# A segment-maximum product on the full array in place of two column halves

## The chip, the cores and the metric

One core of one Trainium2 chip runs the whole kernel. The time is the device time of one execution, in microseconds (us). Each matmul engine instruction is seen in the profile as a weight load (PEld) and a matmul (PE); an f32 product is two such pairs.

## The reference

A graph layer over 12,500 nodes and 400,000 edges, the edges sorted by their target node. `h` is the layer norm of `x` clipped at zero; every edge passes source features, target features and its own features through a two-layer perceptron, and each node takes the maximum over its incoming edges.

```python
h = jnp.maximum(_layernorm(x, axis=-1), 0.0)
e_feat = jnp.concatenate([h[src], h[dst], edge_attr], axis=-1)   # 400000 x 96
v = jax.nn.relu(e_feat @ W1 + b1) @ W2 + b2                      # 96 -> 64 -> 32
x_cand = jax.ops.segment_max(v, dst, num_segments=12500)
out = x + jnp.maximum(x_cand, h)
```

## The kernel before

The edges are cut into four stripes (NS = 4) and each stripe into 196 chunks of C = 512 edges. A chunk is worked on for all four stripes at once; since the target nodes are sorted, the edges of one stripe in one chunk fall into a window of W = 32 consecutive nodes, whose first node is known beforehand.

The main loop takes two chunks a pass (c and c + 1), 98 passes. While it finishes chunks c and c + 1, it gathers the source rows of chunks a = c + 2 and b = c + 3. In a chunk, 12 groups of 128 source rows come by indirect DMAs issued by POOL (line 156, 24 a pass), and four groups come by `tile`: 14 matmuls of a one-hot matrix against the node table `hs` (line 240), a masked product and a maximum on DVE (lines 244 and 245). `to_features` transposes both kinds into `ht` on DVE (lines 258 and 261). A gathered row group lies in one of 24 buffers, three groups each, and a buffer comes free with the transpose.

The first layer sums three products into the four PSUM tiles `ph` (line 502: edge features, target windows, source rows, each a 64-row half of the array); ACT applies the relu (line 557); the second layer is line 573, written into two column halves of a PSUM tile `pv`. DVE scans along the edges of each stripe with add and max (line 580), so that at the last edge of every node stands that node's maximum.

`leave_1` and `leave_2` take these maxima out. `lasts` (line 470) makes, for every block of 128 edges (J = 4 of them), a 0/1 matrix `last` of 128 edges by 4 stripes by 32 window places: one where the edge is the last of its node. `leave_1` transposes the scan result to edges by (4 stripes x 32 features) (line 478) and adds the bias (line 480), giving `so`. `leave_2` multiplies `last` with `so` (line 488), so that each window place gets its node's maximum, copies the result to `wo` on ACT (line 492) and writes four pieces of 32 nodes by 32 features to `top_d` (line 496). Stripes 0 and 2 go to one table, 1 and 3 to the other, and the end of the kernel takes the larger.

Every engine but POOL works in the order written out by hand. On PE a pass reads: tile(a, 0), source-row products, tile(a, 1), tile(a, 2), edge products, second layer, window products, the deferred `leave_2` of the odd chunk of the pass before, tile(a, 3), transposes, tile(b, 0), `leave_2` of chunk c, tile(b, 1), transposes, tile(b, 2), tile(b, 3). The PSUM tiles `pv` come from one pool of three buffers that `tile`, the second layer, `leave_1` and `leave_2` use in turn. SP's queue carries the window loads `qw` (line 457), the edge features and the write-outs of `wo`, in the order of the program.

Of the kernel before, what the change touches and what calls it, by code (L numbers as in the profile page):

```python
# [8 lines left out]
F32 = mybir.dt.float32  # L9
# [14 lines left out]
P = 128  # L24
N = 12500
E = 400000
D = 32
# [3 lines left out]
NS = 4  # L31
W = 32
C = 512
J = C // P
# [33 lines left out]
def gnn_kernel(ctx, tc, x, src, src_mm, src_t, dst, dst_ext, lo, lo_c, ends_b, edge_attr, weights, w1, w2, b2, out):  # L68
# [19 lines left out]
    nc = tc.nc  # L88
# [7 lines left out]
    top_d = [dram.tile([NP, D], F32, name=f"top_d{k}") for k in range(2)]  # L96
# [66 lines left out]
    early_ps = ctx.enter_context(tc.tile_pool(name="early_ps", bufs=1, space=PSUM))  # L163
# [265 lines left out]
    with tc.tile_pool(name="edges", bufs=3) as pool, tc.tile_pool(name="edges_ps", bufs=1, space=PSUM) as ps:  # L429
# [37 lines left out]
        def lasts(c):  # L467
            last = pool.tile([P, J, NS, W], F32, name="last", bufs=2)
            at = ats[c // BLOCK].rearrange("p (s c) j -> p s c j", s=NS)[:, :, c % BLOCK].rearrange("p s j -> p j s")
            nc.vector.tensor_tensor(last, count_ps[:, None, None, :].to_broadcast([P, J, NS, W]),  # L470
                                    at[:, :, :, None].to_broadcast([P, J, NS, W]), op=ALU.is_equal)
            return last

        def leave_1(c, sm):

            px = early_ps.tile([P, C], F32, name="pv", bufs=3).rearrange("p (j q) -> p j q", j=J)
            for j in range(J):
                nc.tensor.transpose(px[:, j, :], sm[:, j * P:(j + 1) * P], ident)
            so = pool.tile([P, J, P], F32, name="so", bufs=2)
            nc.vector.tensor_tensor(so, px, b2r[:, None, :].to_broadcast([P, J, P]), op=ALU.add)  # L480
            return so

        def leave_2(c, so, last):

            pw = early_ps.tile([P, C], F32, name="pv", bufs=3)[:, :2 * D]
            for j in range(J):
                for g in range(2):
                    nc.tensor.matmul(pw[g * 2 * W:(g + 1) * 2 * W],  # L488
                                     last[:, j, 2 * g:2 * g + 2].rearrange("p s w -> p (s w)"),
                                     so[:, j, g * 2 * D:(g + 1) * 2 * D], start=(j == 0), stop=(j == J - 1))  # L490
            wo = pool.tile([P, 2 * D], F32, name="wo")
            nc.scalar.activation(wo, pw, AF.Copy)  # L492
            _, base = windows.pop(c)
            for s in range(NS):
                g = slice(s * W, (s + 1) * W)
                nc.sync.dma_start(top_d[s % 2][bass.ds(base[s], W), :], wo[g, s % 2 * D:(s % 2 + 1) * D])

        def into_ph(ph, pairs, start, stop):
            for x, (w, e) in enumerate(pairs):
# [35 lines left out]
        for c in range(0, NCH, 2):  # L535
# [32 lines left out]
            last = [lasts(c)]  # L568
            ph = edges_into(a)
            pv = [early_ps.tile([P, C], F32, name="pv", bufs=3) for x in range(2)]  # L570
# [15 lines left out]
            so = leave_1(c, sms[0])  # L586
            last.append(lasts(c + 1))
            tile(b, 0)
            to_features(b, 0)
            one_hots(a + 2, 0, 2)  # L590
            leave_2(c, so, last[0])
            tile(b, 1)
            to_features(b, 1)
            so = leave_1(c + 1, sms[1])
# [11 lines left out]
            if c == (NB - 1) * BLOCK:  # L606
# [7 lines left out]
                nc.tensor.matmul(bp, worst, ones, start=True, stop=True)  # L614
                nc.vector.tensor_copy(general_i, bp)
            leave = lambda c=c + 1, so=so, last=last[1]: leave_2(c, so, last)
        leave()

# [154 lines left out]
```

## Time and profile before

| what | value |
|---|---|
| median of 3 runs | 4055.93 us (4045.58 to 4070.74) |
| the profiled execution, its time | 4066.76 us |
| its span, first to last instruction | 4065.0 us |
| mean granted PE clock | 0.939 |
| busy PE, PEld, DVE, ACT, POOL | 3500.2, 2584.2, 2232.7, 1106.1, 2257.0 us |
| line 488 on PE: 3136 matmuls | 166.1 us busy, 232 ns each |
| line 492 on ACT: 196 copies | 43.8 us busy, 223 ns each |

Busy time counts an engine as busy while an instruction of it is in flight. Matmuls overlap, so the mean time of one is longer than the distance from one to the next; where that distance matters, it is read from the starts in the timeline. An idle time is put down to the event that ended it; "issue" means that the profile shows no such event.

### The profile page before, as it was taken

Reading aid. Unit: us, or ns where it says so; the run is one execution under the profiler, and the core shown is the slowest. Engines: PE = TensorE matmul, PEld = TensorE weight load, DVE = VectorE, ACT = ScalarE, POOL = GpSimd, SP = SyncE. Lnnn points to the kernel's source line nnn. Section 1 sums busy time; section 2 is a strip of 40 time slices with the busy share of each in tenths; the row PEclk is TensorE's granted clock in tenths of the full one; section 3 lists DMA queues with packets and bytes.
Section 4 is the critical chain, followed back from the end, with each engine's and each line's share of the span. In section 5 each row is a group of like instructions: output and inputs, shape, how many; then the busy total and the mean of one; then the engine's idle time right before and its main releaser. Section 6 shows DMA issues by size and latency. Waiting matters only on the chain. (4 is left out here: it accounts for less than half of the span.)

```text
span 4065.0 us, 52812 instructions
## 1 busy us (share of the span) xinstructions
PE 3500.2 (86%) x18053; PEld 2584.2 (64%) x18053; DVE 2232.7 (55%) x3876; ACT 1106.1 (27%) x1795; POOL 2257.0 (56%) x2376
## 2 busy tenths in 40 slices
PE   4688889888888898888988888998888889998896
PEld 3466666666666666666666666666666666666665
DVE  4355556555555555555555555555555555655555
ACT  3122222222222222222222232322222223222231
POOL 6555555555555556555555555555555555555550
PEclk7799999999999999999999999999999999999998
DMA  5122212211222122111322222222122222211221
GB/s 189 46 48 65 52 44 55 68 43 44 54 65 49 44 51 69 46 44 46 71 49 47 62 58 47 44 70 52 44 46 66 53 47 49 70 48 44 57 59 50
DMA packets 188622, 229.27 MB, mean 56 GB/s; under 512 B 117549, under 2 KB 159933, under 8 KB 175550
## 3 DMA queue, kind: packets, MB, share of 16 engines
q10 hardware_dynamic: 26692, 110.63, 8.7%
q1 hardware_dynamic: 86618, 76.67, 7.7%
q0 software_dynamic: 75040, 38.57, 6.3%
q8 instruction: 143, 2.34, 0.2%
q14 instruction: 129, 1.06, 0.1%
HBM read 211.76 MB, written 13.85 MB: 56 GB/s over the span
## 5 line engine op out<-in xcount | busy, mean ns | idle before, releaser
L156 POOL DMA_INDIRECT gh<-h_d,src_i x2345 | 2236.5, 954 | 1685.9 <-issue 619.2
L240 PE MATMUL pv<-hs,hot 128*128 128x448 f32 x10920 | 2434.7, 378 | 231.8 <-issue 166.7
L240 PEld LDWEIGHTS pv<-hs,hot 128*128 128x128 f32 x10920 | 2077.6, 194 | 509.9 <-issue 258.1
L244 DVE TENSOR_TENSOR one<-pv,mask 128x448 f32<-128x448 f32 x780 | 478.3, 613 | 1590.8 <-remote 653.4
L557 ACT ACTIVATE hid<-ph,wt 128x512 f32<-128x512 f32 x392 | 254.6, 686 | 1498.2 <-PE ph L502 920.7
L209 DVE TENSOR_TENSOR hot<-kb,consts 128x1536 fp32r<-128x1536 f16 (+2 forms) x388 | 566.1, 1459 | 0.0
L245 DVE TENSOR_REDUCE gm<-one 128x32 f32<-128x448 f32 x780 | 483.6, 620 | 26.9
L219 ACT ACTIVATE hot<-away,ones 128x512 fp32r<-128x512 f32 x392 | 283.6, 724 | 337.3 <-issue 326.3
L580 DVE TENSOR_TENSOR_SCAN sm<-pb,sm,pv 128x512 f32<-128x512 bf16 x195 | 248.2, 1273 | 150.5 <-remote 114.7
L492 ACT ACTIVATE wo<-pv 128x64 f32<-128x64 f32 x196 | 43.8, 223 | 1052.8 <-PE pv L488 765.0
L573 PE MATMUL pv<-hid,wt 128*64 128x512 f32 x784 | 242.1, 667 | 62.2 <-issue 36.3
L488 PEld LDWEIGHTS pv<-so,last 128*64 128x64 f32 x3136 | 126.0, 140 | 250.7 <-issue 162.0
L488 PE MATMUL pv<-so,last 128*64 128x64 f32 x3136 | 166.1, 232 | 131.9 <-issue 121.7
L218 ACT ACTIVATE away<-kb,key_n 128x512 f32<-128x512 f16 x392 | 277.7, 708 | 0.0
L502 PE MATMUL ph<-ea,wt 64*128 64x512 f32 x784 | 233.8, 632 | 35.2 <-issue 29.8
L502 PE MATMUL ph<-ht,wt 64*128 64x512 f32 x784 | 209.7, 637 | 48.3 <-DVE ht L261 42.7
L258 DVE STREAM_TRANSPOSE ht<-gh 128x96 f32<-128x96 f32 x782 | 209.7, 268 | 0.0
L502 PE MATMUL ph<-of,qw 64*128 64x512 f32 x784 | 206.0, 635 | 2.8 <-issue 2.7
L573 PEld LDWEIGHTS pv<-hid,wt 128*64 128x64 f32 x784 | 57.1, 143 | 235.2 <-issue 161.4
L502 PEld LDWEIGHTS ph<-of,qw 64*128 64x128 f32 x784 | 71.9, 195 | 145.4 <-issue 139.3
L502 PEld LDWEIGHTS ph<-ea,wt 64*128 64x128 f32 x784 | 78.3, 188 | 129.5 <-issue 116.2
L502 PEld LDWEIGHTS ph<-ht,wt 64*128 64x128 f32 x784 | 65.2, 188 | 138.2 <-DVE ht L261 77.8
(78 smaller groups left out, 1014.1 us busy)
## 6 DMA issues: line engine op xcount, KB each, us to landing
ea<-in_edge_attr SPq DMA_DIRECT2D x49, 1024.0 KB
db<-in_dst_ext ACTq DMA_DIRECT2D x48, 1024.0 KB
gh<-h_d,src_i POOLq DMA_INDIRECT x2345
pb<-pen_d ACTq DMA_DIRECT2D x48, 512.0 KB
kb<-key_d ACTq DMA_DIRECT2D x47, 512.0 KB
qw<-q_d SPq DMA_DIRECT2D x784, 8.0 KB
top_d<-wo SPq DMA_DIRECT2D x784, 4.0 KB
top_d<-zero ACTq DMA_DIRECT2D x2, 1568.0 KB
```

Of the source, the lines that this page charges most:

```text
L156: nc.gpsimd.indirect_dma_start(out=parts[-1][:, i, :], out_offset=None, in_=h_d[:, :], in_offset=bass.IndirectOffsetOnAxis(ap=src_i[:, c, ...
L209: nc.vector.tensor_tensor(hot_of(c)[:, start:stop], keys[c][:, None, :].to_broadcast([P, n, MM * P]), key_ps[:, start:stop, None].to_broad ...
L218: nc.scalar.activation(away, keys[c], AF.Square, bias=key_n[:, k:k + 1])
L219: nc.scalar.activation(hot_of(c)[:, k], away, AF.Relu, bias=ones, scale=-1.0)
L240: nc.tensor.matmul(po, hot[:, k, e], hs[:, part, k].rearrange("p f a -> p (f a)"), start=(k == 0 and part == 0), stop=(k == A1 - 1 and par ...
L244: nc.vector.tensor_tensor(one, of_group, masks[c][:, m, None, :].to_broadcast([P, D, A0]), op=ALU.mult)
L245: nc.vector.tensor_reduce(mm_rows[c][:, m, :], one, axis=AX.X, op=ALU.max)
L488: nc.tensor.matmul(pw[g * 2 * W:(g + 1) * 2 * W], last[:, j, 2 * g:2 * g + 2].rearrange("p s w -> p (s w)"), so[:, j, g * 2 * D:(g + 1) * ...
L502: nc.tensor.matmul(ph[2 * x + k], w[g], e[g], start=start, stop=stop)
L557: nc.scalar.activation(hid[s], ph[s], AF.Relu, bias=b1c)
L573: nc.tensor.matmul(pv[x][k * 2 * D:(k + 1) * 2 * D], w2x, hid[2 * x + k], start=True, stop=True)
L580: nc.vector.tensor_tensor_scan(sm, loaded.pop(c + x)[2], pv[x], before, op0=ALU.add, op1=ALU.max)
```

## The change

`leave_2` is rewritten. Before, two products per block of 128 edges, each for a pair of stripes, with 64 stationary columns and 64 moving columns, write the lower and the upper half of a 128 x 64 result. After, one product per block takes all four stripes: 128 stationary columns (4 stripes x 32 places) and 128 moving columns (4 stripes x 32 features). Of the 128 x 128 result only the four 32 x 32 blocks on the diagonal, a stripe's places with the same stripe's features, are wanted; the others are copied along and not written out. `wo` becomes 128 x 128 and has two buffers in place of the pool's three. The products of the first and second layer, with their block-diagonal weights, are as before.

```diff
         def leave_2(c, so, last):
-            pw = early_ps.tile([P, C], F32, name="pv", bufs=3)[:, :2 * D]
+            pw = early_ps.tile([P, C], F32, name="pv", bufs=3)[:, :NS * D]
             for j in range(J):
-                for g in range(2):
-                    nc.tensor.matmul(pw[g * 2 * W:(g + 1) * 2 * W],
-                                     last[:, j, 2 * g:2 * g + 2].rearrange("p s w -> p (s w)"),
-                                     so[:, j, g * 2 * D:(g + 1) * 2 * D], start=(j == 0), stop=(j == J - 1))
-            wo = pool.tile([P, 2 * D], F32, name="wo")
+                nc.tensor.matmul(pw, last[:, j].rearrange("p s w -> p (s w)"), so[:, j],
+                                 start=(j == 0), stop=(j == J - 1))
+            wo = pool.tile([P, NS * D], F32, name="wo", bufs=2)
             nc.scalar.activation(wo, pw, AF.Copy)
             _, base = windows.pop(c)
             for s in range(NS):
                 g = slice(s * W, (s + 1) * W)
-                nc.sync.dma_start(top_d[s % 2][bass.ds(base[s], W), :], wo[g, s % 2 * D:(s % 2 + 1) * D])
+                nc.sync.dma_start(top_d[s % 2][bass.ds(base[s], W), :], wo[g, s * D:(s + 1) * D])
```

## The prediction

> **What bounds the kernel now.** I read the busy table first, then the groups of instructions, then the timeline of single passes, engine by engine, then a table by stage.
>
> ```profile
> PE 3500.2 (86%) x18053; PEld 2584.2 (64%) x18053; DVE 2232.7 (55%) x3876; ACT 1106.1 (27%) x1795; POOL 2257.0 (56%) x2376
> L488 PEld LDWEIGHTS pv<-so,last 128*64 128x64 f32 x3136 | 126.0, 140 | 250.7 <-issue 162.0
> L488 PE MATMUL pv<-so,last 128*64 128x64 f32 x3136 | 166.1, 232 | 131.9 <-issue 121.7
> ...
> L492 ACT ACTIVATE wo<-pv 128x64 f32<-128x64 f32 x196 | 43.8, 223 | 1052.8 <-PE pv L488 765.0
> ```
>
> By its share PE looks like the bound, and the edited product is 166 us of it, 4% of the span. The next table sets four passes of the main loop (two chunks each, from one tile(a, 0) to the next) side by side; columns are the stretch, its length, busy time (instructions) of PE, PEld, DVE, ACT and POOL, then PE clock, DMA share, GB/s.
>
> ```profile
> 1605.50:1650.30 44.80, 37.92 (x186) 28.26 (x186) 22.20 (x40) 10.90 (x18) 22.86 (x25) 0.89 0.28 68
> 1650.30:1687.70 37.40, 33.87 (x185) 25.34 (x184) 22.16 (x40) 11.21 (x18) 23.24 (x26) 1.00 0.17 34
> 2017.30:2056.80 39.50, 36.54 (x185) 25.96 (x185) 21.99 (x39) 11.20 (x18) 22.84 (x25) 0.96 0.31 74
> ...
> 3956.00:3988.60 32.60, 32.60 (x185) 25.04 (x184) 22.29 (x38) 10.88 (x18) 0.00 (x0) 1.00 0.02 4
> ```
>
> The instructions are the same in all four, yet the pass takes 32.6 us at full PE once the gathers have ended (last row, POOL x0) and 37.4 to 44.8 us beside them. So PE bounds only the last passes. In the others 5 to 12 us are spent waiting, and the timeline shows where. PE (start, length, then engine, line, operation, tiles, shapes, count):
>
> ```profile
> 2045.23 0.69 PE L488 MATMUL pv<-so,last 128*64 128x64 f32 x16
> 2045.85 3.08 PE L240 MATMUL pv<-hs,hot 128*128 128x448 f32 x14
> 2048.77 0.60 PE L478 MATMUL pv<-ident,sm 128*128 128x128 f32 x4
> ```
>
> POOL:
>
> ```profile
> 2050.95 0.95 POOL L156 DMA_INDIRECT gh<-h_d,src_i  x1 [0.30 <-issue]
> 2054.94 0.95 POOL L156 DMA_INDIRECT gh<-h_d,src_i  x1 [3.03 <-DVE ht L258]
> ```
>
> DVE, where the bracket gives the idle time before the instruction and who ended it:
>
> ```profile
> 2053.21 0.62 DVE L244 TENSOR_TENSOR one<-pv,mask 128x448 f32<-128x448 f32 x1 [4.95 <-PE pv L240]
> ```
>
> tile(b, 1) (14 matmuls from 2045.85) is through PE by about 2049, but DVE gets it only at 2053.21, 1.3 us after the train of six gathers (2044.68 to 2051.90) ends; DVE then frees gather buffers and the next train starts at 2054.94. This repeats: PE's completions come through late while POOL issues gathers back to back, 1.26 us each, and 24 gathers a pass make 30.2 us of the 39. The ring that sets the pass is thus POOL train, late completion, DVE (L244, L245, L258), next train. leave_2 is on PE, beside this ring.
>
> **The change part by part.** leave_2 runs twice a pass: once in place for chunk c (between tile(b, 0) and tile(b, 1)), once deferred for the odd chunk (after the window products, before tile(a, 3)).
>
> *Matmuls.* Each f32 matmul is two instructions. Before: 16 a chunk, two column halves side by side, 0.62 us from the first to the next tile's first (2045.23 to 2045.85). Its two changes of array shape also cost the neighbours: tile, leave_2, tile from 2042.24 to 2048.77 is 6.53 us. Streaming, the tiles' matmuls start 0.201 us apart, so 28 are 5.62 us, and 0.1 us of the first tile's row lies under the transposes before it: leave_2 costs 6.53 - 5.62 - 0.10 = 0.81 us. After: 8 of 128x128 with 128 columns moving, in the shape of the tiles around. No row has this product. Nearest are the head's L364, full array, f32, 256 columns, 0.216 us apart when streaming (so 0.108 for 128), and the transposes L478 (four of 128x128, 0.355 us from start to next start, 0.09 each).
>
> ```profile
> 27.70 1.98 PE L364 MATMUL pp<-wt,hq 128*128 128x256 f32 x8
> ```
>
> Bounds: 8 x 0.09 = 0.72 us if they stream like the transposes; 8 x 0.216 = 1.73 us if the loading of 128 f32 columns does not hide behind a product this short. I take 8 x 0.108 = 0.86, because in L364 the weight load fits beside the matmul and only the columns set the pace. In place: 0.86 - 0.81 = +0.05 us (-0.1 to +0.9). Deferred: it follows 64-row products, so one change of shape stays, and only 0.1 us is saved beside it: 0.86 - 0.62 = +0.25 us (+0.1 to +1.1).
>
> [...]
>
> *What hides them.* In place: DVE took tile(b, 1) at 2053.21, over 4 us after PE had it, so +0.05 is covered; uncovered, 98 x 0.05 = +5 us. Deferred: after it tile(a, 3) waits for the scan to free its PSUM buffer (0.33 us idle before 2038.97). Over the trace, in 48 of 94 passes the deferred product and this wait together take 1.3 to 3 us, in 23 over 3 us, and only in 23 under 1.3 us. I count a quarter of 98 passes as exposed: 25 x 0.25 = +6 us; uncovered everywhere, +25 us.
>
> *Issue.* 16 weight loads and 16 matmuls a chunk become 8 and 8. In the smooth passes this is worth nothing; in the slow ones it is a rival below.
>
> *wo.* The copy takes 128x128 in place of 128x64: 223 ns for 64 columns and 686 for 512 (L557) put it at 223 + 64 x 1.03 = 290 ns, +0.07 us on ACT, 27% busy. Its PSUM buffer is needed two tiles later, some 3 us off. Not on the path: 0 (uncovered, 196 x 0.07 = +13 us). With two buffers in place of three, a copy waits for the write-out of two chunks before, about 39 us back; the four 4 KB writes issue within 3.3 us (SP's timeline at 1630.07). SP's queue loads the windows of later chunks ahead of them and its longest wait there is 12.3 us (L457 for db), well under 39. 0; if it did bind, ACT's copy would hold one_hots_act behind it.
>
> *Output DMAs.* Same number, size and order; only the source slice moves. 0.
>
> **Sum.** +6 (deferred) + 0 (in place) + 0 (wo) + 0 (DMAs) = +6 us. The profiled execution took 4066.8 us (span 4065.0); it would become 4073. That execution lies 10.8 us above the median of the three runs shown, 4055.9, so on the median the forecast is **4062 us**, no change within 1%.
>
> **Rivals.**
>
> *A. Fewer instructions shorten the slow passes: faster.* In 23 of 94 passes the deferred product is torn apart. The timeline of one:
>
> ```profile
> 1623.66 0.25 PE L488 MATMUL pv<-so,last 128*64 128x64 f32 x1 [0.27 <-issue]
> ...
> 1624.37 0.13 PEld L488 LDWEIGHTS pv<-so,last 128*64 128x64 f32 x1 [0.60 <-issue]
> 1625.09 0.22 PE L488 MATMUL pv<-so,last 128*64 128x64 f32 x1 [1.17 <-issue]
> ...
> 1629.43 2.66 DVE L580 TENSOR_TENSOR_SCAN sm<-pb,sm,pv 128x512 f32<-128x512 bf16 x2 [5.13 <-remote]
> ...
> 1630.77 5.60 PE L240 MATMUL pv<-hs,hot 128*128 128x448 f32 x14 [1.04 <-DVE sm L580]
> ```
>
> From the ninth matmul on, PE issues one instruction per 0.7 us during a train of gathers; the product lasts 6.5 us, and the tile after it runs at half clock (5.60 against 3.08 us). These passes take about 44.7 us, and the passes ahead of them 37.4, as in the table. With eight matmuls the product would be issued before the slow stretch begins. If the completions that the scan waits for then come earlier, each pair falls from 82.1 to two passes of 39.3: 3.5 us x 23 = -81 us, some 3980. Against it: the scan started at 1629.43, 1.8 us after the train's last gather ended (1627.59), so the train, not the product, seems to let it go.
>
> *B. Longer trains: slower.* The train after tile(a, 3) has six gathers when tile(b, 1) reaches DVE after its end (2053.21 above), nine when it does before; the trace has 26 nine-gather trains in 92 passes, and most lead to a slow pass next. Where the product in place ends relative to the train decides. If tile(b, 1) is released earlier (16 fewer instructions ahead of it), more passes go that way, at most every second one: 49 pairs, 23 more than now, x 3.5 = +80 us, 4136. It costs over 1% from 12 more pairs on (12 x 3.5 = 42, 4098). For it: these passes come from a difference of 0.8 us in start. Against: a later tile(b, 1), by +0.05, pushes the other way.
>
> *C. The product shows: slower.* Weight loads not hidden, +0.9 us in place and +1.1 deferred; with the covers above eating half, 98 x 1.0 = +98 us, 4154. L364 speaks against it.
>
> *D. The change does nothing that counts,* the sums being equal: inside the forecast.
>
> **How the numbers follow.** Forecast with D 0.46, A 0.25, B 0.17, C 0.12. One per cent (40 us) is about what a measurement of this kernel can tell from no change. So faster 0.25, same 0.46, slower 0.29. The forecast's own range is 4040 to 4095. The 8-in-10 range reaches past A's 3980 and through nearly all of B, and leaves out C: 3970 to 4135.
>
> **What would show it.** Right: eight L488 matmuls of 128*128 taking 0.8 to 0.95 us in place, 14 tile matmuls after them without the 0.1 us of a shape change; passes still of 37, 39 and 45 us; DVE L244 still released 1 to 2 us after trains; the last passes, PE-bound, longer by about 0.3 us. Wrong: L488 near 1.7 us (C); few or no torn products and 45 us passes gone (A); many more nine-gather trains (B); ACT L492 waiting on write-outs.

## The result, and the profile after

The changed kernel takes 4337.5 us (median of four runs, 4306.6 to 4347.0) against 4050.8 us for the kernel before (four runs, 4036.1 to 4070.7): a ratio of 1.068 (1.063 to 1.073). It is slower by 287 us where no change was forecast. Its profiled execution has a span of 4335.2 us, 270 us more than before, at a mean granted PE clock of 0.899 (0.939 before).

The page of after, the busy table and the groups that answer to those shown of before:

```profile
PE 3547.2 (82%) x16485; PEld 2709.8 (63%) x16485; DVE 2254.5 (52%) x3876; ACT 1110.5 (26%) x1795; POOL 2258.1 (52%) x2376
...
L156 POOL DMA_INDIRECT gh<-h_d,src_i x2345 | 2237.6, 954 | 1952.5 <-DVE ht L261 818.4
L240 PE MATMUL pv<-hs,hot 128*128 128x448 f32 x10920 | 2511.6, 387 | 591.8 <-DVE sm L578 514.1
...
L490 ACT ACTIVATE wo<-pv 128x128 f32<-128x128 f32 x196 | 54.3, 277 | 1247.5 <-remote 884.3
...
L487 PEld LDWEIGHTS pv<-so,last 128*128 128x128 f32 x1568 | 197.9, 192 | 99.3 <-issue 66.1
L487 PE MATMUL pv<-so,last 128*128 128x128 f32 x1568 | 217.8, 282 | 21.0 <-issue 10.2
```

The edited product is seen to be small: 52 us more busy time on PE, and ACT's copy at 277 ns. POOL's row is the one to read, beside the same two rows of before:

```profile
L156 POOL DMA_INDIRECT gh<-h_d,src_i x2345 | 2236.5, 954 | 1685.9 <-issue 619.2
L240 PE MATMUL pv<-hs,hot 128*128 128x448 f32 x10920 | 2434.7, 378 | 231.8 <-issue 166.7
```

POOL was as busy before (2236.5 us) but idle for 1685.9 us ahead of its gathers, now for 1952.5: 267 of the 270 us are there, and most of this idle time ends with DVE's transposes, which free gather buffers. And the tiles on PE (L240), which had waited 231.8 us, wait 591.8, of which 514.1 for DVE's scan (`sm`, L578).

Pass by pass (distance between one in-place copy to `wo` and the next, 90 passes), the mean went from 40.3 to 43.2 us. Before, 23 passes took 43 us or more; after, 64. The table by stage shows four passes of after (columns as before):

```profile
1962.20:2003.50 41.30, 36.74 (x169) 28.37 (x168) 21.45 (x39) 11.10 (x18) 22.89 (x25) 0.92 0.30 75
...
2048.00:2092.50 44.50, 36.40 (x170) 28.19 (x170) 22.34 (x38) 11.10 (x18) 22.82 (x24) 0.88 0.26 63
2225.90:2265.80 39.90, 35.38 (x169) 26.74 (x169) 23.70 (x44) 11.10 (x18) 23.09 (x25) 0.96 0.29 72
4220.00:4253.00 33.00, 33.00 (x170) 25.98 (x168) 22.14 (x39) 10.99 (x18) 4.80 (x1) 1.00 0.05 15
```

Without gathers a pass needs 33.0 us of PE, 0.4 more than before. Beside them passes of 40 and 44.5 us remain, as before; but the short ones of 37 us, nearly all, have gone, and the longest have become the rule. The timeline of the 44.5 us pass says how. PE:

```profile
2065.15 1.16 PE L487 MATMUL pv<-so,last 128*128 128x128 f32 x8
2073.87 5.60 PE L240 MATMUL pv<-hs,hot 128*128 128x448 f32 x14 [7.56 <-DVE sm L578]
...
2082.73 1.05 PE L487 MATMUL pv<-so,last 128*128 128x128 f32 x8
2083.54 3.06 PE L240 MATMUL pv<-hs,hot 128*128 128x448 f32 x14
2086.43 0.60 PE L478 MATMUL pv<-ident,sm 128*128 128x128 f32 x4
```

POOL, the first and last gather of one train and some of the next:

```profile
2051.26 0.95 POOL L156 DMA_INDIRECT gh<-h_d,src_i  x1 [3.58 <-DVE ht L258]
...
2068.83 0.95 POOL L156 DMA_INDIRECT gh<-h_d,src_i  x1 [0.30 <-issue]
2081.24 0.95 POOL L156 DMA_INDIRECT gh<-h_d,src_i  x1 [11.45 <-DVE ht L261]
...
2087.51 0.95 POOL L156 DMA_INDIRECT gh<-h_d,src_i  x1 [0.30 <-issue]
2088.77 0.95 POOL L156 DMA_INDIRECT gh<-h_d,src_i  x1 [0.30 <-issue]
...
2091.28 0.95 POOL L156 DMA_INDIRECT gh<-h_d,src_i  x1 [0.31 <-issue]
2095.83 0.95 POOL L156 DMA_INDIRECT gh<-h_d,src_i  x1 [3.60 <-DVE ht L258]
```

DVE:

```profile
2072.53 2.66 DVE L578 TENSOR_TENSOR_SCAN sm<-pb,sm,pv 128x512 f32<-128x512 bf16 x2 [6.53 <-remote]
...
2086.90 0.62 DVE L244 TENSOR_TENSOR one<-pv,mask 128x448 f32<-128x448 f32 x1 [1.41 <-issue]
2087.56 0.62 DVE L245 TENSOR_REDUCE gm<-one 128x32 f32<-128x448 f32 x1
2088.10 0.27 DVE L258 STREAM_TRANSPOSE ht<-gh 128x96 f32<-128x96 f32 x1
```

Read them from the end of the pass. The train that starts at 2081.24 has buffers for six gathers; the sixth starts at 2087.51. tile(b, 1), on PE from 2083.54 to about 2086.4, reaches DVE at 2086.90, and at 2088.37 DVE has freed a buffer of three groups, just before POOL would have run out. So the train goes on without a pause to a ninth gather. In the pass shown of before, tile(b, 1) reached DVE 1.3 us after the end of the train of six. The next train then starts not ahead of tile(a, 0) of the next pass but 3.3 us behind it (2051.26 against 2048.00 in the pass above), twelve to fifteen gathers long. In that pass the second layer is issued by 2063.3, while the train runs to 2069.78; the scan gets it at 2072.53. tile(a, 3) waits 7.56 us for the scan and then runs at half pace (5.60 us against 3.06, at a granted clock of 0.50 from 2073.87 to 2079.30). Its completion brings the next train at the same place again.

Nine-gather trains follow the transposes of the first chunk in 86 of 92 passes; before, in 26. Where the time went, by the mean distance from the first matmul of a stage to the first of the next (85 passes, before, then after): deferred product and the wait behind it 3.44, 6.90 us; tile(a, 3) 3.69, 4.67; source-row products 2.58, 3.39; product in place 0.62, 0.81. Other waits got shorter, since one long wait has taken their place: second layer 2.97, 1.92; edge products 2.74, 2.03; tile(b, 2) 3.35, 2.89. Over all stages, those not named here too, the sum is +3.0 us a pass.

### The profile page after: what moved, and what is told of

It is laid out like the page before. It is cut to its first block, busy times and chain, and to the rows that moved or that the text cites. A ratio compares the mean times of both kernels' runs of the same rounds, so it can differ in the third digit from the quotient of the medians.

```text
span 4335.2 us, 49725 instructions
## 1 busy us (share of the span) xinstructions
PE 3547.2 (82%) x16485; PEld 2709.8 (63%) x16485; DVE 2254.5 (52%) x3876; ACT 1110.5 (26%) x1795; POOL 2258.1 (52%) x2376
## 5 line engine op out<-in xcount | busy, mean ns | idle before, releaser
L156 POOL DMA_INDIRECT gh<-h_d,src_i x2345 | 2237.6, 954 | 1952.5 <-DVE ht L261 818.4
L240 PE MATMUL pv<-hs,hot 128*128 128x448 f32 x10920 | 2511.6, 387 | 591.8 <-DVE sm L578 514.1
L240 PEld LDWEIGHTS pv<-hs,hot 128*128 128x128 f32 x10920 | 2155.3, 202 | 869.5 <-DVE sm L578 530.3
L578 DVE TENSOR_TENSOR_SCAN sm<-pb,sm,pv 128x512 f32<-128x512 bf16 x195 | 249.2, 1278 | 466.0 <-remote 450.1
L490 ACT ACTIVATE wo<-pv 128x128 f32<-128x128 f32 x196 | 54.3, 277 | 1247.5 <-remote 884.3
L500 PE MATMUL ph<-ht,wt 64*128 64x512 f32 x784 | 232.2, 675 | 97.6 <-DVE ht L261 97.6
L487 PEld LDWEIGHTS pv<-so,last 128*128 128x128 f32 x1568 | 197.9, 192 | 99.3 <-issue 66.1
L487 PE MATMUL pv<-so,last 128*128 128x128 f32 x1568 | 217.8, 282 | 21.0 <-issue 10.2
L500 PE MATMUL ph<-ea,wt 64*128 64x512 f32 x784 | 209.8, 626 | 20.0 <-issue 18.0
L571 PE MATMUL pv<-hid,wt 128*64 128x512 f32 x784 | 196.2, 620 | 0.0
L480 DVE TENSOR_TENSOR so<-pv,wt 128x512 f32<-128x512 f32 x196 | 131.5, 671 | 96.2 <-PE pv L240 73.8
L464 ACT ACTIVATE of<-db,below 128x512 f32<-128x512 int32 x196 | 140.0, 714 | 19.9 <-issue 19.9
```

The costliest lines, as they stand in the source:

```text
L156: nc.gpsimd.indirect_dma_start(out=parts[-1][:, i, :], out_offset=None, in_=h_d[:, :], in_offset=bass.IndirectOffsetOnAxis(ap=src_i[:, c, ...
L240: nc.tensor.matmul(po, hot[:, k, e], hs[:, part, k].rearrange("p f a -> p (f a)"), start=(k == 0 and part == 0), stop=(k == A1 - 1 and par ...
L487: nc.tensor.matmul(pw, last[:, j].rearrange("p s w -> p (s w)"), so[:, j], start=(j == 0), stop=(j == J - 1))
L500: nc.tensor.matmul(ph[2 * x + k], w[g], e[g], start=start, stop=stop)
L578: nc.vector.tensor_tensor_scan(sm, loaded.pop(c + x)[2], pv[x], before, op0=ALU.add, op1=ALU.max)
```

## The experiments

The question was why tile(b, 1) comes to DVE sooner, when its matmuls are no earlier. Three theories stood against each other. *Number:* 16 fewer PE instructions between the train's first gather and tile(b, 1)'s last matmul bring its completion out sooner, as if only so many could be handled beside gathers. *Time:* what counts is when PE has done it. *The deferred product:* it is no longer torn, and that shifts the rest. A fourth, that DVE itself starts late beside the gathers, can be ruled out from the trace of before. In the pass shown, PE's records of tile(b, 1), the transposes and tile(b, 2) end at 2048.93, 2049.37 and 2052.18, but the semaphore events by which PE reports them stand at 2053.18, 2053.25 and 2053.39, nearly together, and DVE starts at 2053.21. In 89 of 95 passes DVE takes tile(b, 1) within 0.03 us of such an event; in the other 6 the trace holds no event for it. So it is PE's report that is late.

In what follows a pass of 43 us or more is a long pass; each ratio is to the kernel before on the same chip. The first four ran on one chip (7), the others on chips 10, 11 and 4, and the chip turned out to matter.

**One place at a time.** `e1_halves_in_place` puts the column halves back between tile(b, 0) and tile(b, 1) and leaves the deferred product on the full array; `e2_halves_deferred` is its mirror image.

```diff
-        def leave_2(c, so, last):
+        def leave_2(c, so, last, halves):
+            if halves:
+                ...  # as before the change, 16 matmuls of 64 columns
+            else:
+                ...  # as after it, 8 of 128
...
-            leave_2(c, so, last[0])
+            leave_2(c, so, last[0], True)     # e2: False
...
-            leave = lambda c=c + 1, so=so, last=last[1]: leave_2(c, so, last)
+            leave = lambda c=c + 1, so=so, last=last[1]: leave_2(c, so, last, False)     # e2: True
```

> The changed kernel with the product in place (between tile(b, 0) and tile(b, 1)) put back to two column halves, 32 PE instructions (weight loads and matmuls); the deferred one stays on the full array, 16 instructions; wo keeps 128 columns and two buffers. Theory N (number): a train of gathers lets about 64 PE instructions through promptly. In the two traces tile(b, 1) reaches DVE before the end of the train of six whenever at most 59 PE instructions lie between the train's first gather and its last matmul (before: 3 of 3, after: 87 of 90), in 23 of 38 passes with 63, and in none of 50 passes with 67 or more. The change took 16 out of that stretch. Theory N expects this kernel back near 4050 us (4000 to 4110), about a quarter to a third of the trains with nine gathers. Rival S (the full-array product itself, or the wider copy and two wo buffers, wherever it stands): half or all of the loss stays, 4190 to 4340 us. Rival L (the deferred product is what costs): 4340 us.

> The mirror image: the product in place on the full array, 16 PE instructions; the deferred one in two column halves, 32 instructions. Theory N expects the whole loss, 4300 to 4350 us, with nine-gather trains in nearly every pass. Rival S expects half, about 4190 us. Rival L expects 4050 us.

e1 took 4101.6 us (4078.1 to 4142.2), 1.015 (1.010 to 1.021), with 28 long passes in the trace, which is of its shortest run. e2 took 4340.2 us, 1.072 (1.067 to 1.076), with 65. The loss is with the product in place. Both keep `wo` at 128 columns with two buffers, so these are not what costs. And in e2 the deferred product is torn again, as the trace shows:

```profile
2019.36 0.50 PE L489 MATMUL pv<-so,last 128*64 128x64 f32 x9
2021.03 0.22 PE L489 MATMUL pv<-so,last 128*64 128x64 f32 x1 [1.16 <-issue]
...
2026.63 0.26 PE L489 MATMUL pv<-so,last 128*64 128x64 f32 x1 [1.02 <-issue]
2028.02 5.34 PE L240 MATMUL pv<-hs,hot 128*128 128x448 f32 x14 [1.13 <-DVE sm L587]
```

One or two matmuls at a time over 7.5 us, and then tile(a, 3) waits for the scan just the same. Torn or whole, such a pass takes 44 to 45 us. The third theory falls.

**The number put back, at another pace.** `e3_full_split` keeps the full array but cuts the moving columns into two of 64, so that the product has its 32 PE instructions again.

```diff
-            for j in range(J):
-                nc.tensor.matmul(pw, last[:, j].rearrange("p s w -> p (s w)"), so[:, j],
+            for k, j in [(k, j) for k in range(2) for j in range(J)]:
+                r = slice(k * P // 2, (k + 1) * P // 2)
+                nc.tensor.matmul(pw[:, r], last[:, j].rearrange("p s w -> p (s w)"), so[:, j, r],
                                  start=(j == 0), stop=(j == J - 1))
```

> The changed kernel, full array in both places, but each product's 128 moving columns go in two matmuls of 64, so that a product is again 32 PE instructions, now all of 128x128 weights. It is more work for PE than either kernel: 16 weight loads of 128 columns, about 16 x 0.107 = 1.7 us where the weight loads set the pace, against 0.81 and 0.62. Theory N expects 4050 us or less (3950 to 4110), although PE does about 1 us more per product, because tile(b, 1) again lies behind more than 64 instructions. A rival by time (tile(b, 1) has to end early or late, whatever the number of instructions): it ends 0.9 us later than in the changed kernel. In before it ended 4.3 or 5.1 us after the train's first gather, in the changed kernel 5.2 us; by time alone this kernel would keep the changed kernel's 4340 us or add to it, 4340 to 4500. Rival S: 4340 us or more.

4137.4 us, 1.018 (1.014 to 1.023), 30 long passes. Most of the loss is gone although the product in place now takes 1.70 us. But it also lasts 0.9 us longer, so number and time were not told apart yet.

**More instructions in the kernel before.** `e4_before_64_in_place` cuts before's product in place into moving parts of 32 columns: 64 instructions in place of 32.

```diff
-            for j in range(J):
+            for k, j in [(k, j) for k in range(parts) for j in range(J)]:   # parts: 2 in place, 1 deferred
+                r = slice(k * 2 * D // parts, (k + 1) * 2 * D // parts)
                 for g in range(2):
-                    nc.tensor.matmul(pw[g * 2 * W:(g + 1) * 2 * W],
+                    nc.tensor.matmul(pw[g * 2 * W:(g + 1) * 2 * W, r],
...
-                                     so[:, j, g * 2 * D:(g + 1) * 2 * D], start=(j == 0), stop=(j == J - 1))
+                                     so[:, j, g * 2 * D:(g + 1) * 2 * D][:, r],
+                                     start=(j == 0), stop=(j == J - 1))
```

> The kernel before, with the product in place cut further: the moving 64 columns of each half go in two matmuls of 32, so 64 PE instructions in place of 32; the deferred one is as before. Theory N expects that no train is released early any more: before had 26 nine-gather trains in 92 passes, each pair of passes with one about 3.5 us longer, so -26 x 3.5 = -91 us, 3960 us (3930 to 4010). If the number has nothing to do with it, the product only gets longer by up to 0.5 us where it may be hidden: 4050 to 4100 us.

4038.6 us, 0.997 (0.995 to 0.999). As expected, tile(b, 1) is never released during the train, no train of fifteen is left, and 6 long passes remain of 23. The time, however, missed: the 3960 that this should have given is not there. The product's own completion now comes late as well: the copy to `wo` follows its last matmul by 4.1 us, 0.9 before, and tile(b, 2) waits for this copy, which frees its buffer. From the second transposes to tile(b, 2) it is 1.2 us a pass longer; the product in place takes 0.5 and the edge products 0.4 us longer. Against that, the deferred product and the wait behind it are 1.7 us shorter. What the long passes lost is spent on waits in all passes.

**Something else ahead of tile(b, 1).** `e5_before_px_first` and `e6_after_px_first` move the transposes of the second chunk (four transposes, eight instructions) from behind tile(b, 1) to ahead of it, in before and in after.

```diff
             leave_2(c, so, last[0])
+            so = leave_1(c + 1, sms[1])
             tile(b, 1)
             to_features(b, 1)
-            so = leave_1(c + 1, sms[1])
```

With them `e7_before_no_gather` and `e8_after_no_gather` take the gathers away.

```diff
-            for i in range(min(SOME, n - k)):
-                nc.gpsimd.indirect_dma_start(
-                    out=parts[-1][:, i, :], out_offset=None, in_=h_d[:, :],
-                    in_offset=bass.IndirectOffsetOnAxis(ap=src_i[:, c, k + i:k + i + 1], axis=0))
+            nc.gpsimd.memset(parts[-1], 0.0)
```

> The kernel before, with the transposes of the second chunk (leave_1, four matmuls, 8 PE instructions) put ahead of tile(b, 1) in place of behind it, on PE and DVE alike. No work is added. The stretch from the train's first gather to tile(b, 1)'s last matmul grows from 63 or 71 PE instructions to 71 or 79, while the product in place keeps its place (the kernel with 64 instructions in the product had no early release and few slow passes, but there the product itself came out late and tile(b, 2) waited 1.2 us a pass). Theory N expects no early release, slow passes of 43 us and over down from 23 to 10 or fewer, and a time below before: 3960 to 4030 us. Without it, the order is neutral: 4040 to 4080 us.

> The changed kernel with the same move: 8 PE instructions more ahead of tile(b, 1)'s end, so 63 in the passes that had 55, at the border where before and the two split kernels show both outcomes. Theory N expects a mixture and a time between: early releases in a half to nine tenths of the passes, 4120 to 4300 us. If the full array itself costs the time, 4340 us.

> The kernel before with the gathers left out: each group of three gathers is one short memset on POOL, so that the edges of those rows get zeros for source features; everything else is as it was. Theory N says that the passes are long only beside trains of gathers, so all passes become like the last ones of the trace, 32.7 us: 98 x 32.7 + 190 us ahead of and behind the loop = 3390 us.

> The same for the changed kernel (gathers left out). Its last passes take 33.1 us, so 98 x 0.4 = 40 us more than the kernel before without gathers, 3430 us: what the change costs by PE alone, about 1%. If the full-array product costs the 280 us by itself, the distance to the kernel before without gathers stays near 280 us.

These four met a chip (10) on which the kernel before takes 3297.0 us (3293.1 to 3301.8), not 4050. e5 took 3293.2, 0.9985 (0.9976 to 0.9994); e6 3334.9, 1.011 (1.010 to 1.013); e7 3297.1, 1.000 (0.999 to 1.001); e8 3337.2, 1.012 (1.010 to 1.014). Nothing is held back there. The page of e5:

```profile
PE 3221.1 (98%) x18053; PEld 2478.2 (75%) x18053; DVE 2248.8 (68%) x3876; ACT 1090.2 (33%) x1795; POOL 2258.5 (69%) x2376
```

PE is busy for 98% of the span beside the same 2258 us of gathers. In the stretch shown gathers follow one another from 2005.31 to past 2032.95, and tile(b, 0) reaches DVE in the midst of them (PE, then DVE), as tile(b, 1), on PE from 2007.74 to about 2010.6, does at 2010.84:

```profile
2003.73 3.06 PE L240 MATMUL pv<-hs,hot 128*128 128x448 f32 x14
```

```profile
2006.83 0.62 DVE L244 TENSOR_TENSOR one<-pv,mask 128x448 f32<-128x448 f32 x1 [0.42 <-PE pv L240]
```

So the four say nothing on the theories, but two other things well: e7 equals before, so on this chip gathers cost nothing; and the change costs PE alone 3337.2 - 3297.1 = 40 us, 0.41 us a pass.

**The same on a chip that holds back.** On chip 11, `e9_before_px_first` (the kernel of e5), `e10_after_px_first` (that of e6), `e11_after_again` (the changed kernel as it is) and `e12_before_no_gather` (that of e7) ran together.

> The same kernel as e5 (before, with the transposes of the second chunk ahead of tile(b, 1)) once more, because e5's runs were on a chip on which before itself takes 3297 us, every pass 32.7 us, and no completion is held back beside gathers; there the question could not arise. On a chip on which before takes about 4056 us, theory N (about 64 PE instructions come through promptly from a train's first gather on) expects no early release with 71 or 79 instructions, at most 10 passes of 43 us and over in place of 23, and 3960 to 4030 us; without it 4040 to 4080 us. On a chip of the other kind: 3293 us again.

> The same kernel as e6 (changed, with the same move, 63 instructions where there were 55), for the same reason. On a chip on which before takes about 4056 us, theory N expects early releases in a half to nine tenths of the passes and 4120 to 4300 us; 4340 us if the full array itself costs the time. On a chip of the other kind: 3335 us again.

> The changed kernel itself, beside before on whichever kind of chip this is. Where before takes about 4056 us: 4340 us, as measured. Where before takes 3297 us, passes are bound by PE, so only PE's own cost is left, 98 x 0.4 us = 40 us: 3337 us, +1.2%.

> The same kernel as e7 (before with the gathers left out, zeros in place of the gathered source features). On a chip on which before takes about 4056 us, theory N and every theory by which the trains of gathers hold PE back expect 3300 us, a fifth less; if such a chip were slower for another reason, the time would stay well above 3300 us. On a chip of the other kind: 3297 us again.

Before took 4045.4 us there (4029.4 to 4074.5), e12 3297.3, a ratio of 0.815 (0.810 to 0.821): on this chip a fifth of the kernel's time goes with the gathers. The changed kernel took 4159.0, 1.028 (1.022 to 1.033), less than half the loss of the first result, with 34 long passes. With eight instructions more ahead of tile(b, 1), e10 took 4054.2 (4012.6 to 4075.1), 1.002 (0.999 to 1.005), with 6 in the trace, which is of its shortest run: the loss is gone. The same move in before gave nothing, 4046.3, 1.001 (0.998 to 1.003), although its trace has only 8 long passes (no trace of before was taken on this chip); the second layer and the window products take 4.5 and 3.5 us in place of the 1.9 that each needs, and the 3960 to 4030 expected was missed in the manner of e4.

The same kernel on two chips, POOL's row of e5 (chip 10) and of e9 (chip 11):

```profile
L156 POOL DMA_INDIRECT gh<-h_d,src_i x2345 | 2237.9, 954 | 911.8 <-issue 606.1
```

```profile
L156 POOL DMA_INDIRECT gh<-h_d,src_i x2345 | 2235.5, 953 | 1675.3 <-DVE ht L258 670.2
```

A gather costs POOL the same 0.95 us; what differs is how long POOL waits for its buffers.

**Number against time.** On chip 4, `e13_after_wide` keeps after's 16 instructions in place but lets each matmul move 256 columns (the product twice, the second copy unused), 0.73 us longer (0.81 became 1.54). `e14_before_trace` and `e15_after_beside` are before and after as they are, and `e16_after_px_beside` is the kernel of e10.

```diff
+            if wide:                        # in place; the deferred product as after
+                pd = early_ps.tile([P, C], F32, name="pv", bufs=3)[:, :2 * NS * D]
+                for j in range(J):
+                    nc.tensor.matmul(pd.rearrange("p (k f) -> p k f", k=2), last[:, j].rearrange("p s w -> p (s w)"),
+                                     so[:, j, None, :].to_broadcast([P, 2, NS * D]), start=(j == 0), stop=(j == J - 1))
+                pw = pd[:, :NS * D]
```

> The changed kernel with each of the four matmuls in place given its moving columns twice over (256 in place of 128; the second copy of the result is not read). The number of PE instructions stays 16; the product takes 8 x 0.216 = 1.73 us in place of 0.81, as long as the one of the split kernel e3, which had 32. Theory N expects the changed kernel's behaviour: early releases as often as there (beside it in this set), and its time or some 0.9 us a pass more, where not hidden: 0 to +90 us against e15. A theory by time expects e3's behaviour: few early releases and 80 to 200 us less than e15 on a chip that holds completions back. On a chip that holds nothing back: 98 x 0.9 = 90 us more than e15.

> The kernel before, unchanged, for its trace on the same chip as the other three. On a chip where it takes about 4050 us: mostly late releases with 63 and 71 instructions, as in the first trace, or all late if this chip lets fewer than 63 through, as the chip of e9 to e12 may do (there 63 and more were always late, 55 mixed, 47 and fewer early). Otherwise 3297 us.

> The changed kernel, unchanged, on the same chip as e13, e14 and e16: 4150 to 4340 us where before takes about 4050 us, by theory N the more, the more of its passes with 55 instructions come early; 3337 us where before takes 3297 us.

> The changed kernel with the transposes of the second chunk (8 PE instructions) ahead of tile(b, 1), beside the three others. Theory N expects it below e15 on a chip that holds completions back: about the time of before, as on the chip of e9 to e12, if 63 instructions are mostly late there, and between the two if they are mixed. Without theory N it equals e15.

Before took 4056.1 us on this chip (4027.1 to 4090.5), e14 4065.8 in its one run, with 24 long passes. e15 took 4343.9, 1.071 (1.062 to 1.080), 63 long passes: the first result once more. e13 took 4134.2, 1.019 (1.009 to 1.028), 38 long passes; e16 4105.9, 1.011 (1.007 to 1.015), 40. 400 us of e15 and of e16, by the table of stages:

```profile
2000.00:2400.00 400.00, 329.72 (x1530) 252.73 (x1530) 204.34 (x351) 101.64 (x165) 208.65 (x219) 0.89 0.23 50
```

```profile
2000.00:2400.00 400.00, 341.97 (x1626) 260.15 (x1625) 214.31 (x371) 107.95 (x175) 221.09 (x233) 0.94 0.24 53
```

In the same time e16 does 1626 matmuls and 233 gathers, e15 1530 and 219: 6% more work, at a higher granted clock (0.94 against 0.89), with no instruction of PE removed.

e13 speaks against a pure count: same number as e15, later end, and most of the loss gone. The traces of all these kernels, taken together, show how number and end go together. For every pass, count the PE instructions (weight loads and matmuls) from the first gather of the train of six to tile(b, 1)'s last matmul, and note when that matmul ends and when DVE takes the tile, both from the first gather on. The end is taken as the last matmul's start plus 0.2 us, the distance of two matmuls; the ranges leave out up to three passes of a row. The sixth gather ends 7.2 us after the first, and DVE needs 1.5 us more to free a buffer, so only a release by about 6.0 us makes the train nine long: in these traces every nine-gather train at this place has its release by 6.1 us. The last column counts a little more widely, all releases by 7.0 us.

| kernel (chip) | PE instructions | ends at, us | DVE takes it at, us | by 7.0 us |
|---|---|---|---|---|
| before | 63 | 4.1 | 4.3 to 8.6 | 23 of 38 |
| before | 71 | 4.9 | 7.1 to 8.6 | none of 42 |
| after | 55 | 5.0 | 5.2 to 6.0 | 68 of 70 |
| e1 (7) | 63 | 4.2 | 4.3 to 8.5 | 15 of 18 |
| e1 (7) | 71 | 4.9 | 7.0 to 8.6 | none of 39 |
| e2 (7) | 55 | 5.0 | as after | 82 of 84 |
| e3 (7) | 63 | 5.2 | 5.5 to 6.4 | 30 of 33 |
| e3 (7) | 71 | 5.9 | 7.4 to 9.0 | none of 42 |
| e14, before (4) | 63 | 4.1 | 4.3 to 8.6 | 23 of 30 |
| e14, before (4) | 71 | 4.9 | 7.1 to 8.6 | none of 49 |
| e15, after (4) | 55 | 5.0 | as after | 68 of 69 |
| e13 (4) | 47 | 5.2 | 5.4 to 5.7 | all 26 |
| e13 (4) | 55 | 5.8 | 6.0 to 7.6 | 11 of 53 |
| e16 (4) | 55 | 4.8 | mostly 5.0 to 6.0 | 18 of 20 |
| e16 (4) | 63 | 5.4 | mostly late | 10 of 46 |
| e11, after (11) | 55 | 5.0 | 5.2 to 7.4 | 41 of 63 |
| e10 (11) | 55 | 4.8 | early and late | 13 of 45 |
| e10 (11) | 63 | 5.4 | 7.3 to 8.8 | none of 37 |
| e9 (11) | 71 | 4.6 | 8.6 to 8.9 | none of 30 |
| e9 (11) | 79 | 5.3 | 8.6 to 8.8 | none of 41 |

At equal end the number decides: 71 instructions ending at 4.9 are never out in time, 55 ending at 5.0 nearly always (e1 and e2 on chip 7, e14 and e15 on chip 4). At equal number the end can decide: 55 ending at 5.0 against 55 ending at 5.8 (e15 and e13, chip 4); of e13's early ones only 5 came by 6.1 us and made the train nine long. On these two chips the delay from the end to DVE grows with the number: 0.2 to 0.5 us at 47, mostly up to 1.0 at 55 when it ends early and up to 1.8 when late, 0.2 to 4.4 at 63, 1.5 to 3.7 at 71. What counts is end plus delay against some 6 us. The change took 16 instructions out of this stretch, 71 to 55 in the passes that had been late, left the end where it was, 4.9 to 5.0, and so moved the release from behind the train's end to ahead of it.

The two figures are not the whole rule: with 63 instructions e3, which ends at 5.2, is out by 7.0 us in 30 of 33 passes, before, which ends at 4.1, in only 23 of 38, and e16, which ends at 5.4, in 10 of 46.

What stays open: why the delay grows with the number, what else it depends on, why chip 11 starts to be late at 55 and chip 10 never, whether POOL's issuing of gathers or their transfers hold PE's reports back (e12 takes both away), and 1.5% of e1, where the deferred product alone is on the full array: PE's share of it is at most 0.30 us x 98 = 29 us, and 28 long passes against 23 (at 5 us each) would be 25 more. Together these come near the 46 us between the medians, but it is not shown that they are it.

## Why the prediction was wrong

*The costs on PE were right.* In place the product was to take 0.86 us in place of 0.81, +0.05. Measured from tile(b, 0)'s first matmul to the end of tile(b, 1)'s stretch, 2.99 + 0.62 + 2.92 = 6.52 us became 2.90 + 0.81 + 2.90 = 6.60, +0.08. Deferred, the forecast was +0.25: 0.615 became 0.914 where nothing stands in the way, +0.30. ACT's copy takes 277 ns, forecast 290. The last passes are longer by 0.4 us, forecast 0.3; 0.38 x 98 is 37 us a run, and e8 against e7 show 40. Rival C's exposed weight loads, +2 us a pass, are not there.

The prediction put 0.81 - 0.62 = 0.19 us of the halves' cost on their two changes of shape. The traces show 0.11 of it: tile(b, 0) lasts 2.90 us in place of 2.99 now that no change follows it, and tile(b, 1) 2.90 in place of 2.92 now that none comes ahead of it.

*The step that failed is "Issue".* "In the smooth passes this is worth nothing": it has no term in the sum, and it was most of the effect, since with the 16 instructions back in place alone (e1) the loss falls from 7% to 1.5%. Sixteen instructions fewer ahead of tile(b, 1) decide whether its completion comes out in time to lengthen the train of six: from the train's first gather on, DVE took the tile at 7.1 to 8.6 us with 71, and takes it at 5.2 to 6.0 with 55.

*The cover of the product in place was read as slack.* "DVE took tile(b, 1) at 2053.21, over 4 us after PE had it, so +0.05 is covered." The 4 us were not spare time in which any change could hide; they were a delay that depends on what lies ahead on PE, and that kept the kernel in its shorter rhythm. Removing the delay made the pass longer.

*Rival B had the mechanism and the direction, and the wrong ceiling.* It named the longer trains, their cause and 16 fewer instructions as what could trigger them, though it had the end of the product decide, and this end hardly moved (4.9 to 5.0). Three parts of it failed. "At most every second one": it took a nine-gather train to be followed by a train of another kind, since before's traces show them in pairs of 45 and 37 us. But a long train leads to a late scan, which leads to the same start of the next one; the state repeats itself, in 86 of 92 passes. "49 pairs, 23 more than now, x 3.5 = +80 us": there are 41 more long passes, and the mean over all passes went up by 2.85 us, 268 us over the 94 passes compared, nearly the whole of the 270 us between the two profiled executions. The pairing had made its price too small as well: it set a long pass of 45 us off against one of 37, and the short ones went. "A later tile(b, 1), by +0.05, pushes the other way": true in sign (e13 shows it, at +0.7 us), but 0.05 us is nothing against the 2 us or so by which 16 instructions move the release.

*Rival A fell as well.* The deferred product is whole in every pass of after, as it foresaw, and the 44 us passes did not go; its own counter-argument, that the train and not the product lets the scan go, fits after and e2, which take nearly the same time with the product whole and torn.

*The tell-tales worked.* "Many more nine-gather trains (B)" is what the profile of after shows at a glance, in POOL's timeline and in POOL's idle row.

## What to carry to other kernels

A wait that hides your cost may be the very thing that your edit moves: before counting a term as covered, ask what sets the length of the cover, and what follows if the covered thing came sooner. Where a ring of engines repeats itself, the price of a changed step is not that of one pass but of the rhythm it tips into, so a rival of this kind needs all passes as its upper bound. Here the order of two calls mattered nearly as much as the product: with the transposes ahead of tile(b, 1) the changed kernel went from 4343.9 to 4105.9 us on one chip and from 4159.0 to 4054.2 on another, though on neither was it faster than before; of all versions only e4 and e5 were, by 0.3% and 0.15%, on one chip each.

## What the runs showed of the hardware

Beside back-to-back indirect DMAs from POOL (one per 1.26 us), PE's completions came out late on three of the experiments' four chips: in before, the events of three finished stages stand within 0.21 us, the first 4.3 us after its stage ended. In some stretches PE's instructions start only in steps of 0.7 us, one to three at a time (in before, from 1623.64 to 1629.42). On the fourth chip, in the stretch shown of e5, neither is seen; there DVE takes tile(b, 0) at 2006.83, 0.04 us after PE's row of it ends. One and the same kernel takes 4045 us on chip 11 and 3297 on chip 10, and 3297 on chip 11 too when the gathers are taken away (e12). On chips 4 and 7 the delay grows with the number of PE instructions since the train began: 0.2 to 0.5 us at 47 (e13, chip 4), 1.5 to 3.7 at 71. On these two the releases by 7.0 us give way to late ones between 55 and 71 instructions (e15 68 of 69, e14 none of 49), while chip 11 is late in part at 55 already (e11 41 of 63 by 7.0 us) and chip 10 has no wait of this kind in what is shown; no run here shows the cause.
